# Hand-overs at the stage borders of an eight-stage fused kernel, and a new order of its last stage

## The chip, the cores and the metric

The kernel runs on one core of a Trainium2 chip. The metric is the device time of one execution in microseconds (us), as the median of several runs. The core has five engines that work beside each other, each through its own queue in order: TensorE (PE, matrix products into the accumulator memory PSUM), VectorE (DVE), ScalarE (ACT), GpSimd (POOL) and SyncE (SP, which here only issues DMAs).

## The reference

Input is x of 16 batches of 256 tokens with 128 features, in f32. Eight blocks follow each other, each with a norm before it, and a norm of its result that is added to x:

```python
x = x + _layernorm(_L0_attn_ref(_layernorm(x, axis=-1), ...), axis=-1)
x = x + _layernorm(_L0_ffn_ref(_layernorm(x, axis=-1), ...), axis=-1)
...
x = x + _layernorm(_L3_attn_ref(_layernorm(x, axis=-1), ...), axis=-1)
x = x + _layernorm(_L3_ffn_ref(_layernorm(x, axis=-1), ...), axis=-1)
```

L0 is one attention head and a gated MLP. L1's first half has four layers of local and linear attention with an FFN after each; its second half is a soft mixture of experts (2048 slots, softmax over slots and over tokens). L2 is causal attention and a GELU MLP. L3's first half is a selective scan, an MLP, grouped attention and a second MLP (root-mean-square norms ahead of each); its second half sends each batch's 64 best tokens per expert through 8 experts.

## The kernel before, in words

**Tiles.** The 4096 tokens lie as 8 groups (`NG`) of 512 tokens, two batches each; a group is a tile `x[g]` of 128 partitions x 4 x 128 f32, and x stays in SBUF from start to end. Work per group is written as a Python generator. A `yield` ends a turn of the generator; who runs next decides the order of the instructions in each engine's queue.

**Stages.** `program` calls seven stages, each in its own pools of SBUF and PSUM tiles: `stage_l0`; `stage_l1_attn` (L1's four layers, and in the last of them `fill`, which norms x for the next stage); `stage_soft_moe`; `stage_l2_attn`; `stage_trunk` (L2's MLP, the scan, L3's first MLP); `l3_gqa`; `stage_last` (L3's second MLP for each group, its closing norms, and the experts). A tile of a new pool can be used when the memory under it has been released by the stage before.

**Order.** Within `stage_l0`, the two attention stages, the trunk and the last stage the order is written by hand (`manual_schedule`): `Ctx.turns` (L373) runs items of (first turn, generator), one step of each per turn, in the order of the list. In the L1 stage and the soft mixture the program's own scheduler plans the queues from the traced order; there `Ctx.interleave` (L219) starts L1's 64 steps, a mix or an FFN of one group each, a step after the one before has had 4 (mix) or 2 (FFN) turns.

**Norms.** `Ctx.stats` (L247) takes mean and variance on DVE (bn_stats, bn_aggr, four of each per group) and 1/sqrt on POOL (L244, L245). `Ctx.normed` (L262) applies them with four DVE instructions. Two stages have a variant that applies them on ACT: POOL computes nb = -mean * rs (L577, L578; L1627, L1628), ACT computes x * rs + nb (L583, L1631).

**Stage borders.** In stage 0 every group ends with y (L719), its norm, the add to x, a second norm of x, z = normed x. L1 then begins: it fills its constant tiles on POOL (L746, L748), and the first mix norms z[0], transposes it and scales it (L776) to hT; products with hT follow. At the end of L1, `fill` stores x to DRAM and norms it on DVE into mxn. In the soft mixture the last pass `share` (L1145) collects two token blocks per group; then `end` divides by the sums (L1166, L1168), norms on DVE (mdisp) and adds the stored x back (L1170); it runs inside `share`, so the next block comes after it. The L2 attention starts with a norm of x[0] while POOL fills the value tiles (L344 to L349).

**The last stage.** `last(g)` squares xm[g] on POOL (L1638), sums on DVE (L1641), takes rsqrt on POOL, multiplies (n), transposes, goes through fc (Relu L1656, Square L1657) and proj, adds, norms twice, transposes and multiplies with the gate, and writes the probabilities. `selection(q)` finds the best tokens for four batches (two groups); `pair_of(q, pair)` gathers their tokens ("xin"), runs two experts and adds the results up ("sum"). The turns at which each starts stand in one list:

```python
    items = []
    for q in range(4):
        items += [(25 + 8 * q + 2 * pair, pair_of(q, pair)) for pair in range(4)]
    items = items[::-1] + [((19, 25, 33, 42)[q], selection(q)) for q in range(4)]
    items += [((0, 1, 3, 5, 7, 9, 19, 21)[g], last(g)) for g in range(NG)]
```

Of the kernel before, what the change touches and what calls it, by code (L numbers as in the profile page):

```python
# [21 lines left out]
F32 = mybir.dt.float32  # L22
I32 = mybir.dt.int32
BF16 = mybir.dt.bfloat16
AF = mybir.ActivationFunctionType
# [160 lines left out]
def idle(n):  # L186

    for _ in range(n):
        yield
# [10 lines left out]
class Ctx:  # L200
# [61 lines left out]
    def normed(self, out, src, mv, rs):  # L262
        for k in range(NT):
            self.nc.vector.tensor_scalar(
                out[:, k, :], src[:, k, :], mv[:, k, 0:1], rs[:, k : k + 1], ALU.subtract, ALU.mult
            )

# [275 lines left out]

def stage_l0(k, x, w, wv, wi, z):

# [10 lines left out]
    def constants():  # L556
# [12 lines left out]
        for name in f:  # L569
            v.tensor_scalar(f[name], wi[name], float(np.float32(1.0 / 127.0)), None, ALU.mult)  # L570
            yield

    def stats(src):

        mv, rs = k.stats(src)
        nb = k.t([P, NT], "ln_nb", 6)
        gp.tensor_scalar(nb, mv[:, :, 0], -1.0, None, ALU.mult)  # L577
        gp.tensor_tensor(nb, nb, rs, ALU.mult)  # L578
        return nb, rs

    def normed(out, src, nb, rs):
        for t in range(NT):
            nc.scalar.activation(  # L583
                out[:, t, :], src[:, t, :], AF.Identity, bias=nb[:, t : t + 1], scale=rs[:, t : t + 1]
            )

# [60 lines left out]

    def group(g):
        nb, rs = stats(x[g])
        yield from idle(2)  # L650
        xn = k.t([P, NT, D], "xn", 2)
        normed(xn, x[g], nb, rs)
        yield
# [36 lines left out]
        yield  # L690
        nb, rs = stats(x[g])
        yield from idle(2)
        xn = k.t([P, NT, D], "xf", 2)
        normed(xn, x[g], nb, rs)
        yield
# [21 lines left out]
        ps = k.tokens_ps(h, down)  # L717
        y = k.t([P, NT, D], "y", 3)
        nc.scalar.copy(y, ps)  # L719
        yield  # L720
        mv, rs = k.stats(y)
        yield from idle(2)
        k.normed(y, y, mv, rs)
        gp.tensor_tensor(x[g], x[g], y, ALU.add)
        yield
        nb, rs = stats(x[g])
        yield from idle(2)
        normed(z[g], x[g], nb, rs)
        yield

    with k.tc.manual_schedule():
        k.turns([(0, group(0)), (0, constants())] + [(4 * g, group(g)) for g in range(1, NG)])


def stage_l1_attn(k, x, ws, rows, z, then):

# [8 lines left out]
    for a in k.l1_val + k.l1_lin:  # L745
        nc.gpsimd.memset(a, 1.0)  # L746
    for a in k.l1_max + k.l1_ctx:
# [16 lines left out]
    for i in range(4):  # L764
        steps += [l1_mix(k, z[g], ws[i], rows[f"bo{i}"], NG * i + g) for g in range(NG)]
        steps += [ffn(i, g) for g in range(NG)]
        leads += [4] * NG + [2] * NG
    k.interleave(steps, 5, leads, -1)

# [26 lines left out]

def l1_mix(k, z, w, bo, n):

# [5 lines left out]
    tiles = lambda b: [slice((2 * b + t) * P, (2 * b + t + 1) * P) for t in range(2)]  # L804
    hT = yield from l1_norm_T(k, z, w["ln1_g"], w["ln1_b"])
    nc.gpsimd.tensor_tensor(z, z, bc(bo, 1, NT), ALU.add)
# [145 lines left out]
def soft_inputs(k, x, pool):  # L952

    xs = k.dram.tile([P, NG, NT, D], F32, tag="xs", name="xs")
    xn = [pool.tile([P, NT, D], F32, tag=f"mxn{g}", name=f"mxn{g}") for g in range(NG)]

    def fill(g):
        k.nc.sync.dma_start(out=xs[:, g], in_=x[g])
        yield from k.norm_to(xn[g], x[g])

    return xs, xn, fill


def stage_soft_moe(k, x, w, wdram, bdram, xn, xs):
# [157 lines left out]
    def share(n):  # L1122
# [3 lines left out]
        for b in range(NB):  # L1126
# [15 lines left out]
            for t in range(2):  # L1142
# [3 lines left out]
                else:  # L1146
                    v.tensor_copy(x[g][:, at, :], ps[:, t, 0:D])
            nc.scalar.copy(got[:, :, b], ps[:, :, D])  # L1148
            yield
            if n == blocks - 1 and b % 2:  # L1150
                yield from end(b // 2, f, got)
        if n == 0:
# [5 lines left out]
    def end(g, f, got):  # L1158

        back = k.t([P, NT, D], "slT", 3)  # L1160
        nc.sync.dma_start(out=back, in_=xs[:, g])
        bs = slice(2 * g, 2 * g + 2)
        r = k.t([P, 2, 2], "mend", 2)
        v.tensor_tensor(r, sums[:, :, bs], f[:, :, bs], ALU.mult)
        v.tensor_tensor(r, r, got[:, :, bs], ALU.add)
        v.reciprocal(r, r)  # L1166
        xg = x[g].rearrange("p (b t) d -> p b t d", b=2)
        v.tensor_tensor(xg, xg, bc(r.rearrange("p t b -> p b t"), 3, D), ALU.mult)  # L1168
        n = yield from k.norm(x[g], "mdisp", 3)
        nc.gpsimd.tensor_tensor(x[g], back, n, ALU.add)  # L1170

    for n in range(-2, blocks):
        parts = [
            share(n) if n >= 0 else None,
            logits(n + 2) if n + 2 < blocks else None,
            slots(n + 1) if 0 <= n + 1 < blocks else None,
        ]
        parts = [p for p in parts if p]
        while parts:
            parts = [p for p in parts if next(p, k) is not k]  # L1180


def stage_l2_attn(k, x, w, beside):
# [3 lines left out]
    def head(g, got):  # L1187
        yield
        xn = yield from k.norm(x[g], "xn", 1, 2)
        yield  # L1190
        ps = k.transposed_ps(xn)
# [325 lines left out]
def l3_gqa(k, xa, w, gain, first):  # L1517
# [31 lines left out]
    def tail(g, yT):  # L1549
# [5 lines left out]
        nc.gpsimd.tensor_tensor(xa[g], xa[g], y, ALU.add)  # L1555
        yield

    k.attention_stage(head, 26, 1, tail)
# [54 lines left out]
def stage_last(k, x, xm, w, xn, probs, out):  # L1613
# [9 lines left out]

    def normed(out, src, mv, rs):

        nb = k.t([P, NT], "ln_nb", 3)
        nc.gpsimd.tensor_scalar(nb, mv[:, :, 0], -1.0, None, ALU.mult)  # L1627
        nc.gpsimd.tensor_tensor(nb, nb, rs, ALU.mult)  # L1628
        yield from idle(2)
        for t in range(NT):  # L1630
            nc.scalar.activation(  # L1631
                out[:, t, :], src[:, t, :], AF.Identity, bias=nb[:, t : t + 1], scale=rs[:, t : t + 1]
            )

    def last(g):
        xg = xm[g]
        sq = k.t([P, NT, D], "rms_sq", 2)
        nc.gpsimd.tensor_tensor(sq, xg, xg, ALU.mult)  # L1638
        yield
        ss = k.t([P, NT], "rms_ss", 3)  # L1640
        v.tensor_reduce(ss, sq, AX.X, ALU.add)  # L1641
        rs = k.t([P, NT], "rms_rs", 3)
        k.rsqrt(rs, ss, 1.0 / D, RMS_EPS)
        yield from idle(2)
        n = k.t([P, NT, D], "n", 2)
# [19 lines left out]
        mv, rs = k.stats(y)  # L1665
        yield from idle(2)
        k.normed(y, y, mv, rs)
        nc.gpsimd.tensor_tensor(x[g], x[g], y, ALU.add)
        yield
        mv, rs = k.stats(x[g])  # L1670
        yield from normed(xn[g], x[g], mv, rs)
        yield
# [143 lines left out]
    for q in range(4):  # L1816
        items += [(25 + 8 * q + 2 * pair, pair_of(q, pair)) for pair in range(4)]
    items = items[::-1] + [((19, 25, 33, 42)[q], selection(q)) for q in range(4)]
    items += [((0, 1, 3, 5, 7, 9, 19, 21)[g], last(g)) for g in range(NG)]
    with k.tc.manual_schedule():  # L1820
# [4 lines left out]
def program(ctx: ExitStack, tc: tile.TileContext, xin, dram, at, out):  # L1825
# [45 lines left out]
    k.mhalf = base.tile([P, P], F32, tag="mhalf", name="mhalf")  # L1871
    nc.gpsimd.memset(k.mhalf, -0.5)
    rows1 = load_rows(base, "l1rows")

# [15 lines left out]
    z = [pz.tile([P, NT, D], F32, tag=f"z{g}", name=f"z{g}") for g in range(NG)]  # L1890
    stage("l0", "left", stage_l0, l0, l0v, l0f, z, banks=ONE_RING)
    closed("w0")
# [3 lines left out]
    xs, xn, fill = soft_inputs(k, x, psoft)  # L1896
    stage("l1a", "left", stage_l1_attn, l1, rows1, z, fill, banks=RING_BANKS)
    closed("z")
# [55 lines left out]
```

## Time and profile before

| what | us |
|---|---|
| median of three runs (2999.87 to 3004.17) | 2999.88 |
| the profiled execution | 3001.28 |
| its span | 2999.60 |
| PE busy in the span | 2756.1 (92%) |
| DVE, ACT, POOL busy | 1950.2, 1661.9, 1017.0 |

The stages by their first product on PE, in us of the span: L1 at 190, the soft mixture at 968, the L2 attention at 1564, the trunk at about 1881, the grouped attention at about 2380, the last stage at 2695; PE ends at 2988.

How to read the profile: the page lists busy time per engine and, in 40 slices of 75 us, busy tenths and the granted clock of PE (9 is full or nearly). A row of the timeline has start, length, engine, line, operation, output<-inputs and shapes; "[idle before <-releaser]" says how long the engine had stood and what let it go on. The chain of waits is followed back from the last instruction: each row is start, length, and what the end of the kernel waited for there. The helpers L317 (products) and L306 (transposes) stand for most PE rows; the tile's name says which product it is.

### The profile page before, as it was taken

How to read it: one execution, taken by the hardware profiler on the slowest of the kernel's cores; microseconds unless marked ns; L12 is line 12 of the kernel's file. 1: busy time of each engine (PE TensorE's matmuls, PEld its weight loads, DVE VectorE, ACT ScalarE, POOL GpSimd, SP SyncE). 2: the span in 40 equal slices, each digit the busy share in tenths (PEclk: the TensorE clock that was granted, in tenths of full speed). 3: DMA queues.
4: the chain of work that ended last, by engine and by line, in shares of the span. 5: the costliest groups of instructions: out<-in, count | busy, mean ns of one | idle time of the engine just before them, and what ended most of it. 6: DMA issues, size and time to landing. Idle time of an engine off the chain costs nothing.

```text
span 2999.6 us, 59389 instructions
## 1 busy us (share of the span) xinstructions
PE 2756.1 (92%) x23674; PEld 1881.2 (63%) x23674; DVE 1950.2 (65%) x5342; ACT 1661.9 (55%) x3488; POOL 1017.0 (34%) x1368
## 2 busy tenths in 40 slices
PE   8979999999997799999959998799999699978998
PEld 4547776777666588888843443466666344436897
DVE  5767466564667889999867775566674587735441
ACT  6745556455563667776725665344444277756543
POOL 3453333333335200000044555322231466644332
PEclk9989999999998899999979999899999799988999
DMA  4000000000001000000020000000000000010000
GB/s 115 12 1 2 1 2 2 1 2 1 2 2 37 1 12 12 8 9 9 9 73 1 1 1 1 1 1 1 1 1 1 2 1 1 1 42 16 2 15 15
DMA packets 29149, 31.29 MB, mean 10 GB/s; under 512 B 7292, under 2 KB 20156, under 8 KB 28732
## 3 DMA queue, kind: packets, MB, share of 16 engines
q1 hardware_dynamic: 28872, 27.49, 3.1%
q8 instruction: 187, 3.06, 0.4%
q14 instruction: 90, 0.74, 0.1%
HBM read 23.29 MB, written 4.19 MB: 9 GB/s over the span
## 4 chain that ended last, share of the span: by engine, by line
PE 51%; ACT 7%; DVE 6%; POOL 2%; issue 2%; DMA 0%; POOLq 0%; SPq 0%; ACTq 0%; DVEq 0%
PE ps_s L317 32%; PE ps_o L317 7%; PE ps_mm L317 6%; ACT at_e L472 1%; PE ps_s L306 1%; ACT lg L1129 1%; PE ps_xin L317 1%; ACT meT L1136 1%; PE ps_sum L317 1%; ACT mdisp L1036 1%; ACT lg L1009 1%; PE ps_s L506 1%; PE ps_t L1134 1%; DVE at_nm L440 1%; POOL ln_rs L245 1%
## 5 line engine op out<-in xcount | busy, mean ns | idle before, releaser
L244 POOL TENSOR_SCALAR ln_rs<-ln_mv 128x4 f32<-128x4 f32 x192 | 41.2, 215 | 879.6 <-DVE ln_mv L257 855.1
L440 DVE TENSOR_REDUCE at_nm<-ps_s 128x2 f32<-128x512 f32 (+1 forms) x384 | 238.1, 682 | 123.0 <-PE ps_s L317 123.0
L472 ACT ACTIVATE at_e<-ps_s 128x512 f32<-128x512 f32 x384 | 198.2, 603 | 93.3 <-PE ps_s L317 91.1
L1391 DVE TENSOR_TENSOR scan<-ps_s,lm 128x384 f32<-128x384 f32 x256 | 124.7, 549 | 143.1 <-PE ps_s L317 142.9
L478 POOL TENSOR_SCALAR_AFFINE_SELECT at_e<-at_e 128x1024 f32<-128x1024 f32 (+1 forms) x96 | 135.4, 1411 | 215.0 <-ACT at_e L472 214.7
L245 POOL TENSOR_TENSOR ln_rs<-ln_rs,mhalf 128x4 f32<-128x4 f32 x192 | 196.4, 1023 | 15.7
L854 DVE TENSOR_REDUCE l_max<-ps_s 128x3 f32<-128x384 f32 x256 | 124.1, 548 | 64.0 <-PE ps_s L317 64.0
L317 PE MATMUL ps_o<-my,meT 128*128 128x129 f32 x1024 | 145.6, 290 | 18.3 <-ACT mgot L1148 15.3
L317 PEld LDWEIGHTS ps_s<-l_w,mlp_h 128*128 128x128 f32 x1280 | 149.4, 192 | 18.8 <-issue 15.1
L317 PE MATMUL ps_s<-l1f_phi,mxT 128*128 128x256 f32 x512 | 141.5, 399 | 16.9 <-DVE mpart L1010 16.8
L317 PEld LDWEIGHTS ps_o<-my,meT 128*128 128x128 f32 x1024 | 128.8, 196 | 37.0 <-ACT mgot L1148 21.8
L317 PE MATMUL ps_s<-km,qT 32*128 32x512 f32 x768 | 140.0, 663 | 12.0 <-POOL km L364 10.5
L317 PE MATMUL ps_s<-l_w,mlp_h 128*128 128x128 f32 x1280 | 150.2, 275 | 0.3
L317 PE MATMUL ps_s<-qm,kT 32*128 32x512 f32 x768 | 144.2, 656 | 5.2 <-DVE at_nm L440 5.0
L904 POOL TENSOR_SCALAR_AFFINE_SELECT e<-e 128x512 f32<-128x512 f32 x128 | 78.8, 637 | 178.3 <-ACT e L901 178.3
L317 PE MATMUL ps_o<-at_e,at_vm 128*32 128x128 f32 (+1 forms) x2048 | 122.6, 336 | 15.3 <-ACT at_oT L502 15.3
L317 PE MATMUL ps_mm<-mdisp,mxn 128*128 128x128 f32 x1024 | 125.2, 278 | 5.0 <-DVE mdisp L1048 4.9
L901 ACT ACTIVATE e<-ps_s 128x384 f32<-128x384 f32 x256 | 105.5, 510 | 39.7 <-PE ps_s L317 39.6
L317 PEld LDWEIGHTS ps_mm<-mdisp,mxn 128*128 128x128 f32 x1024 | 121.6, 194 | 7.9 <-DVE mdisp L1048 6.6
L1368 ACT COPY BT<-ps_s 128x512 f32<-128x512 f32 x64 | 37.5, 586 | 154.6 <-PE ps_s L317 154.6
L317 PE MATMUL ps_s<-xT,l_w 128*128 128x512 f32 x256 | 119.3, 596 | 2.7 <-ACT mlp_h L789 2.7
L317 PEld LDWEIGHTS <-b_ident 128*128 128x128 bf16 x656 | 51.5, 98 | 110.0 <-issue 100.2
(427 smaller groups left out, 7083.9 us busy)
## 6 DMA issues: line engine op xcount, KB each, us to landing
mw<-in_l1fw SPq DMA_DIRECT2D x16, 256.0 KB, 2.7
moe_w<-in_moe SPq DMA_DIRECT2D x16, 256.0 KB, 5.3
l_w<-in_l SPq DMA_DIRECT2D x10, 256.0 KB, 3.4
x<-in_x SPq DMA_DIRECT2D x8, 256.0 KB, 4.6
xs<-x SPq DMA_DIRECT2D x8, 256.0 KB, 2.0
slT<-xs SPq DMA_DIRECT2D x8, 256.0 KB, 2.7
out<-x SPq DMA_DIRECT2D x8, 256.0 KB, 2.3
l1f_phi<-in_l1f SPq DMA_DIRECT2D x1, 1024.0 KB, 4.9
```

What stands on the lines that cost most here:

```text
L244: g.tensor_scalar(out, in_, scale, eps, ALU.mult, ALU.add)
L245: g.tensor_tensor(out, out, self.mhalf[:, :n], ALU.pow)
L306: self.nc.tensor.transpose(out[:n, k * P : (k + 1) * P], src[:, k, cols], self.c["ident"])
L317: self.nc.tensor.matmul(out, lhsT=lhsT, rhs=rhs, start=start, stop=stop, skip_group_check=True)
L440: v_.tensor_reduce(nm[:, t, r, vs], s, AX.X, ALU.max, negate=True)
L472: nc.scalar.activation(e[:, r], s, AF.Exp)
L478: nc.gpsimd.affine_select(at, at, [[0, 4], [0, n], [1, P]], ALU.is_ge, 0.0, base=0, channel_multiplier=-1)
L854: v.tensor_reduce(mx[:, b, :, h, 16], s, AX.X, ALU.max, negate=True)
L901: nc.scalar.activation(e[:, h].rearrange("p j n -> p (j n)"), s[:, : 3 * P], AF.Exp)
L904: nc.gpsimd.affine_select(e[:, :, j, :], e[:, :, j, :], [[0, 4], [1, P]], ALU.is_ge, 0.0, base=0, channel_multiplier=-1)
L1368: nc.scalar.copy(s, ps)
L1391: v.tensor_tensor(m, s[:, : SEQ + P], lm[:, SCAN_HEADS[4 * (t // 2) + 2 * i + hh], :], ALU.mult)
```

## The change

Three borders and the last stage are edited. The ACT form of the norm becomes a method of `Ctx`.

```diff
+    def stats_nb(self, src, kept=None):
+        mv, rs = self.stats(src)
+        g = self.nc.gpsimd
+        nb, to = kept or (self.t([P, NT], "ln_nb", 6), rs)
+        g.tensor_scalar(nb, mv[:, :, 0], -1.0, None, ALU.mult)
+        g.tensor_tensor(nb, nb, rs, ALU.mult)
+        if kept:
+            g.tensor_copy(to, rs)
+        return nb, to
+
+    def normed_act(self, out, src, nb, rs):
+        for t in range(NT):
+            self.nc.scalar.activation(
+                out[:, t, :], src[:, t, :], AF.Identity, bias=nb[:, t : t + 1], scale=rs[:, t : t + 1]
+            )
```

Stage 0 to L1: the last group stops at y, which is kept in a tile of its own; the rest of its stage 0 runs beside the first mix of L1. Group 0 also does its first L1 norm and transposes in stage 0. The fills of two kinds of constant tiles, three tiles of each, move from POOL to DVE.

```diff
-        y = k.t([P, NT, D], "y", 3)
+        y = y7 if g == NG - 1 else k.t([P, NT, D], "y", 3)
         nc.scalar.copy(y, ps)
         yield
+        if g == NG - 1:
+            return
...
+        if g == 0:
+            nb, rs = k.stats_nb(z[g])
+            yield from idle(2)
+            xn = k.t([P, NT, D], "xf", 2)
+            k.normed_act(xn, z[g], nb, rs)
+            yield
+            ps = k.transposed_ps(xn)
+            nc.scalar.activation(xT0, ps, AF.Identity, bias=l1["ln1_b"], scale=l1["ln1_g"])
+            yield
...
+def rest_of_l0(k, x, z, y):
+    yield from k.residual(x, y)
+    yield
+    nb, rs = k.stats_nb(x)
+    yield
+    k.normed_act(z, x, nb, rs)
...
     for a in k.l1_val + k.l1_lin:
-        nc.gpsimd.memset(a, 1.0)
+        nc.vector.memset(a, 1.0)
...
+    def beside(a, b):
+        for _ in a:
+            next(b, k)
+            yield
+
+    steps[0] = beside(steps[0], rest_of_l0(k, x[NG - 1], z[NG - 1], y7))
...
-    hT = yield from l1_norm_T(k, z, w["ln1_g"], w["ln1_b"])
+    if hT is None:
+        hT = yield from l1_norm_T(k, z, w["ln1_g"], w["ln1_b"])
```

L1 to the soft mixture: `fill` norms on ACT.

```diff
-        yield from k.norm_to(xn[g], x[g])
+        nb, rs = k.stats_nb(x[g])
+        yield
+        k.normed_act(xn[g], x[g], nb, rs)
```

The soft mixture to L2: `end` becomes a part of its own beside `share`; the division goes into the norm's factor; group 0's next statistics are taken here and kept, and L2 applies them on ACT.

```diff
-            yield
             if n == blocks - 1 and b % 2:
-                yield from end(b // 2, f, got)
+                parts.append(end(b // 2, f, got))
+            yield
...
-        v.reciprocal(r, r)
-        xg = x[g].rearrange("p (b t) d -> p b t d", b=2)
-        v.tensor_tensor(xg, xg, bc(r.rearrange("p t b -> p b t"), 3, D), ALU.mult)
-        n = yield from k.norm(x[g], "mdisp", 3)
-        nc.gpsimd.tensor_tensor(x[g], back, n, ALU.add)
+        rt = k.t([P, NT], "mendt", 3)
+        v.reciprocal(rt.rearrange("p (b t) -> p t b", b=2), r)
...
+        gp.tensor_tensor(rs, mv[:, :, 1], rt, ALU.mult)
+        gp.tensor_tensor(rs, rs, rt, ALU.mult)
+        k.rsqrt(rs, rs, 1.0, LN_EPS)
+        gp.tensor_tensor(rs, rs, rt, ALU.mult)
+        yield
+        n = k.t([P, NT, D], "mdisp", 3)
+        k.normed(n, x[g], mv, rs)
+        gp.tensor_tensor(x[g], back, n, ALU.add)
+        yield
+        if g == 0:
+            k.stats_nb(x[g], k.kept)
...
-        xn = yield from k.norm(x[g], "xn", 1, 2)
-        yield
+        if g == 0:
+            xn = k.t([P, NT, D], "xn", 1)
+            k.normed_act(xn, x[g], *k.kept)
+            yield from idle(3)
+        else:
+            xn = yield from k.norm(x[g], "xn", 1, 2)
+            yield
```

Grouped attention to the last stage: group 0's squares, their sums and the rsqrt are done at the end of that group's attention.

```diff
+        if g == 0:
+            ss = k.t([P, NT], "last_ss", 1)
+            sq = k.t([P, D], "last_sq", 1)
+            for t in range(NT):
+                nc.scalar.activation(sq, xa[g][:, t, :], AF.Square, accum_out=ss[:, t : t + 1])
+            yield
+            k.rsqrt(k.kept[0], ss, 1.0 / D, RMS_EPS)
```

The last stage: `last(0)` starts at the product with the kept factor; three pauses of two turns become one turn (after the rsqrt of the squares, after both statistics); and the list of turns is

```diff
-        items += [(25 + 8 * q + 2 * pair, pair_of(q, pair)) for pair in range(4)]
-    items = items[::-1] + [((19, 25, 33, 42)[q], selection(q)) for q in range(4)]
-    items += [((0, 1, 3, 5, 7, 9, 19, 21)[g], last(g)) for g in range(NG)]
+        items += [(23 + 8 * q + 2 * pair, pair_of(q, pair)) for pair in range(4)]
+    items = items[::-1] + [((16, 21, 30, 38)[q], selection(q)) for q in range(4)]
+    items += [((0, 0, 2, 3, 5, 7, 9, 11)[g], last(g)) for g in range(NG)]
```

## The prediction, made before the change had run

> **What bounds the kernel now.** I read the page's slices first, then the busy time in stretches of 5 us around each low slice, then the chain and the timeline inside those stretches. The page's rows for TensorE and its granted clock:
>
> ```profile
> PE   8979999999997799999959998799999699978998
> PEclk9989999999998899999979999899999799988999
> ```
>
> One digit is 75 us. PE is full nearly everywhere; what is lost lies in a few slices, and in the same slices the clock falls. So the time is PE's work plus the holes at the stage borders, and only holes can be won. Slice 3 (first border), by 5 us, is
>
> ```profile
> 175.00:180.00 5.00, 0.00 (x0) 0.00 (x0) 2.26 (x12) 0.48 (x2) 2.35 (x4) 0.72 0.01 2
> 185.00:190.00 5.00, 0.00 (x0) 0.00 (x0) 2.83 (x21) 0.00 (x0) 4.70 (x14) 0.50 0.00 0
> 195.00:200.00 5.00, 5.00 (x31) 3.17 (x29) 4.91 (x37) 2.10 (x3) 4.50 (x7) 0.74 0.00 0
> ```
>
> After the length of the stretch the columns are PE, its weight loads, DVE, ACT, POOL, the clock, and the DMA. PE stands from 172.6 (last matmul of stage 0) to 190.2 and then works at half clock until about 198. The timeline says why: group 7's chain of norm, add, norm lasts until 183.1; all tiles of the next stage start only then; five us of POOL fills precede the first rsqrt.
>
> The second border, 951 to 968, in the timeline:
>
> ```profile
> 954.87 1.26 POOL L284 TENSOR_TENSOR x<-x,ln_y 128x512 f32<-128x512 f32 x1
> 954.93 2.04 DVE L264 TENSOR_SCALAR mxn<-x,ln_mv,ln_rs 128x128 f32<-128x128 f32 x4 [0.26 <-POOL ln_rs L245]
> 966.08 1.11 DVE L264 TENSOR_SCALAR mxn<-x,ln_mv,ln_rs 128x128 f32<-128x128 f32 x4 [1.42 <-POOL ln_rs L245]
> ```
>
> PE ended its last FFN at 951.1, yet DVE adds that group's result only at 956.9: DVE is two groups late, and each group's mxn occupies it 2.04 us beside POOL's add (1.11 alone). The third border, in the chain:
>
> ```profile
> 1528.65 0.26 DVE x L1145
> ...
> 1529.23 1.24 DVE x L1168
> ...
> 1530.73 0.78 DVE ln_st L255 x4
> ...
> 1532.16 1.03 POOL ln_rs L245
> 1533.25 0.22 issue
> 1533.47 0.85 DVE mdisp L264 x3
> ...
> 1557.27 1.26 POOL x L1170
> ...
> 1562.53 0.99 POOL ln_rs L245
> ```
>
> The middle rows are one group's end. It repeats every 5.75 us (the rsqrt starts at 1526.41, 1532.16, 1537.90, 1543.65), all in series with the next blocks. The last two: the barrier at 1558.5 and the next stage's first norm, whose rsqrt stands behind POOL's fills. In the last stage PE has two holes: 2687.3 to 2695.0, where group 0's square, sum, rsqrt and product follow each other, and
>
> ```profile
> 2760.00:2765.00 5.00, 3.50 (x12) 2.52 (x12) 4.76 (x24) 1.89 (x6) 3.21 (x6) 0.50 0.01 2
> 2765.00:2770.00 5.00, 0.12 (x1) 0.13 (x1) 4.73 (x16) 0.70 (x2) 3.79 (x7) 0.50 0.00 0
> 2770.00:2775.00 5.00, 4.68 (x21) 3.92 (x21) 3.15 (x12) 2.61 (x9) 1.20 (x2) 0.50 0.00 0
> ```
>
> where groups 0 to 5 are through their MLPs and the experts wait for the first selection.
>
> **First border.** Group 7's chain goes beside the first mix; group 0's L1 norm and transposes go into stage 0. PE's first L1 matmul then needs only hT and PSUM, which the copy of y frees at 173.2. SBUF tiles open with the last of group 6, ACT's z at 175.5 instead of 183.1. PE could so start 19 us earlier (192.3 to 173.3). DVE is next: from 175.5 it has six fills (no DVE row; POOL's six take 3 x 0.57 + 3 x 0.31 = 2.6; ends 1.3 and 5; I take 2.6, the same elements), casts 0.6, group 7's two statistics and one norm (1.23 + 1.11 + 1.23 = 3.6), step 0's q 1.15, maxima 3.9 and the rest 2.1, step 1's norm 2.3 and q 1.15: 17.4, to 192.9. Before, step 1's q ended at 209.85, so 16.9; for waits in between I take 16.5 (ends 10 and 21). The fills, moved ahead of everything on DVE's queue, delay the maxima (PE waits for their banks); that is in the sum. With one turn less in step 0, step 1 starts one turn later against it; cover is the 3 us that PE needs for its projections.
> A rule to weigh: "TensorE: Matmul & The Clock Gate" in the Trainium skill (section "What's actually happening") holds that an idle window of about 3.4 us halves the clock and about 3.4 us of work restores it. By that this border's slow restart would cost 1.7 us; by the rows 190 to 200 it costs 3.87 x 0.5 + 5 x 0.26 = 3.2. I use the row; it is inside the 19.
>
> **Second border.** Eight mxn norms go from DVE to ACT: 8 x 2.04 us off DVE, 8 x 1.65 onto ACT (row L583, four in 1.65), and two POOL instructions more (0.23 + 0.20, 0.55 with the gap). After PE's end: add 0.7, statistics 1.2, POOL 1.25, norm 1.1, POOL add 1.26, statistics 1.2, POOL 1.25 + 0.55, ACT 1.65 = 10.2, to 961.3 against 967.2. Group 6's pieces lie between on DVE, so 5.0 (ends -1 and 6). "ScalarE: Activation LUTs" ("Rules for kernel authors") speaks against this: additions and multiplications belong on VectorE, and an ACTIVATE costs about 0.3 us plus 0.83 ns an element, an estimate of 1.6 for four. It is right about the instruction (1.65 against 1.11), and by it alone the border grows by 0.54 + 0.55 = 1.1 us. But the row shows DVE late by 5 us and ACT at 24 of 75 us there, so I follow the row. ACT's Gelu behind it waits up to 1.65 us once per group; in that slice ACT is idle two thirds.
>
> **Third border.** An end loses L1168 (1.24), and its POOL wait (1.44 with its issue) gets the next block's DVE work as cover: DVE's own work is 4 x 0.33 + 3 x 0.16 + 1.2 + 1.1 = 4.1; POOL 3.2 (three products more, 0.6); PE 3.4. I take 4.5 per group, since DVE and POOL block each other now and then (a 128x4 product took 1.12 beside POOL's add). The last rsqrt follows 7 x (5.75 - 4.5) = 8.8 us sooner; last chain about equal. So 9 (ends 3 and 11). SP's loads of xs go with the end into a later turn; behind them on SP wait only weights of later stages and two masks, 2 us to land, so nothing. Then head 0: statistics 1.2, rsqrt 1.0 behind fills, norm 1.3 go; ACT's norm takes 0.5 to the first transpose. POOL's fills (5.8) still end 5.8 after the barrier, and km needs POOL: scores 7.75 after it instead of 12.45: 4.7, of which 4.5. Together 13.5.
>
> **Last border and stage.** Four squares on ACT (no such row; nearest L583, 1.65; between 0 and 1.7) and a rsqrt move into the attention stage, where ACT is busy 55 of 75 us. The chain of POOL, DVE, POOL before the first product goes: 4.8 us sooner on PE. The MLPs: two more groups run in front at the front's rate, 60 us for six heads and three tails of some 51 us of PE work; by that, eight heads and five tails (70 us) take 80 from 2690.2, to 2770. Then the hole stays: the last group's remaining chain (copy 0.6, add 0.7, norm 3.6, add 1.3, norm 4.7, transposes and gate 2.3) is 13.2 us, and this gate stands ahead of the experts' first gather in PE's order, so that starts about 2784.5. After the first gather (2783.6 before) PE ran 203.9 us to 2987.5; 13.6 of that were groups 6 and 7 (one fc, two proj at 3.4, two tails at 1.7) and 1 a selection, so 189.3; the experts' start has no filler now, 4. End 2977.8: 9.7 sooner, I take 8 (ends 2 and 20), as ACT (three copies 1.8, Relu and Square 4 x 1.23, norm 1.65, p 0.4: 8.8 us a group) is as full as PE. The pauses cut from two turns to one cost nothing while a turn of the front lasts 4.4 us (proj starts at 2712.6, 2721.5, 2730.3, two turns apart); without that cover each group would wait 1.25 us for its rsqrt.
>
> **Added in the stages.** Group 0's early norm in stage 0: DVE 1.2, ACT 2.4, POOL 1.7, PE 0.6; covered by 22 of 75 us idle on DVE and 17 on ACT. With the squares 1.5 (ends 0 and 4; a gain is excluded, it is added work).
>
> **Sum.** 16.5 + 5 + 13.5 + 8 - 1.5 = 41.5. The profiled execution took 3001.28 (span 2999.60 and 1.68 around it), 1.4 above the median 2999.88; 3001.3 - 41.5 = 2959.8, on the median's scale 2958.
>
> **Rivals.** (1) As summed: 2958, own range 2947 to 2968, chance 0.60. (2) The hole before the experts closes, because sixteen turns at 5 us leave the selection finished and the first hot rows waiting: the last stage is worth 19, 2947; for it: selection needs two groups only; against: PE's order puts gate 7 first. 0.17. (3) DVE becomes the bound at the borders: fills and late norms push step 0's maxima, the ends run at 5 us: 9 + 3 + 6 + 3 - 1.5 = 19.5, 2980. For it: DVE is at 4.9 of 5 in 195 to 200. 0.16. (4) The release at a border still falls on the same last instruction, so nothing moves: 2998; against: group 7's chain leaves stage 0. 0.03. (5) Slower: L1's order is planned by the program, not written, and a changed start can spread through its 64 steps of (951 - 190)/64 = 11.9 us. A microsecond more per step gives 64 - 41.5 = 22 more, 3022; it turns slower from 0.75 a step. Against: only step 0 differs, and DVE has 47 of 75. 0.04.
>
> **Numbers.** Faster by over 0.2% (about what a measurement here can tell from no change): cases 1 to 3 and a shade, 0.93; within 0.03; slower 0.04. The range 2942 to 2976 leaves out the lower part of (2), half of (3), and (4) and (5): about 0.2.
>
> **What would show it.** PE's gap after stage 0 under 3 us, clock at 1.00 throughout, step 1's q near 193. The second barrier 10 us after PE's last FFN (16 before). Ends 4.5 us apart, no product of 128x512 in them. PE's first transposes of the last stage 1 us after the add; then still a hole near its turn 20. I am wrong if the stretches of L1's inside grow, or if the hole before the experts is gone.

## The result, and the profile after

The changed kernel takes 2980.07 us (median of 4 runs, 2973.4 to 2986.4) where the kernel before took 3000.74 on the same chip (2999.9 to 3004.2): a ratio of 0.9929, 95% interval 0.9905 to 0.9952. It is faster, by 21 us and not by the 41.5 of the forecast. Two later measurements of the same kernel on other chips gave 0.9941 (0.9926 to 0.9956) and 0.9963 (0.9951 to 0.9975), 19 and 11 us. The profiled execution took 2986.44 us (span 2984.7), the slowest of its four, 14.8 below the profiled 3001.28 of before; below, the place of a gain or a loss is read from traces, and its worth is held against the medians of several runs.

The page's rows for TensorE and its granted clock, after:

```profile
PE   8989999999998799999969998799999699989898
PEclk9989999999999799999978999899999799999899
```

The low slices are where they were, only less low: slice 3 (first border) has 8 instead of 7, slice 21 (third border) 6 instead of 5. The three stretches of the first border, in the columns used for before:

```profile
175.00:180.00 5.00, 4.46 (x33) 2.92 (x32) 3.36 (x15) 2.47 (x6) 2.22 (x6) 1.00 0.01 3
185.00:190.00 5.00, 4.06 (x26) 2.54 (x25) 4.94 (x25) 2.02 (x5) 2.40 (x6) 0.50 0.00 0
195.00:200.00 5.00, 5.00 (x13) 2.67 (x11) 3.28 (x15) 2.71 (x6) 3.69 (x5) 0.59 0.00 0
```

TensorE no longer stands: it is busy 4.46 of 5 where it had 0. But DVE is full (4.94 of 5), and the clock is at half from 182 to 199, where 1.00 was expected (a value between 0.50 and 1.00 is a mean over a change: by stretches of 1 us the clock is 1.00 up to 182, then 0.50 up to 199). Step 1's q was forecast to end at 192.9; it ends at 202.4. First TensorE's product that q is made of, then DVE's rows of step 1's norm, of a later step's norm and of q, and last the q of before:

```profile
198.65 2.12 PE L336 MATMUL ps_s<-l_tok,xT 128*128 128x256 f32 x8
```

```profile
190.46 1.29 DVE L264 TENSOR_SCALAR xn<-z,ln_mv,ln_rs 128x128 f32<-128x128 f32 x4 [0.26 <-POOL ln_rs L245]
...
198.39 1.76 DVE L264 TENSOR_SCALAR xn<-z,ln_mv,ln_rs 128x128 f32<-128x128 f32 x4 [1.72 <-POOL ln_rs L245]
...
202.09 0.27 DVE L867 TENSOR_TENSOR q<-ps_s,qm 128x128 f32<-128x128 f32 x1
```

```profile
209.56 0.29 DVE L832 TENSOR_TENSOR q<-ps_s,qm 128x128 f32<-128x128 f32 x1
```

The second border, last rows of POOL's, ACT's and DVE's timelines:

```profile
948.62 1.27 POOL L303 TENSOR_TENSOR x<-x,ln_y 128x512 f32<-128x512 f32 x1
...
954.85 1.81 POOL L1027 MEMSET mdisp<- 128x2048 f32 x1
```

```profile
952.98 1.65 ACT L283 ACTIVATE mxn<-x,ln_nb,ln_rs 128x128 f32<-128x128 f32 x4 [2.62 <-POOL ln_nb L275]
```

```profile
954.85 1.88 DVE L237 COPY mxT<-ps_t 128x512 f32<-128x512 f32 x1
```

TensorE's last FFN ended at 943.5, the barrier falls with ACT's last mxn at 954.6: 11 us instead of 16. Then DVE's first copy and POOL's fill start at the same instant, and the copy takes 1.88 us (the other three take 0.68 to 0.69).

The third border, in the chain of waits, with one whole end between two rsqrt and then the barrier:

```profile
1536.32 1.02 POOL ln_rs L245
...
1537.43 0.20 POOL ln_rs L1217
1537.63 0.03 issue
1537.66 1.11 DVE mdisp L264 x4
1538.77 0.52 DVE x L1182 x2
1539.29 0.84 DVE mend L1203
...
1541.41 0.21 POOL ln_rs L1214
...
1542.25 1.02 POOL ln_rs L245
...
1550.43 1.27 POOL x L1221
1551.71 0.03 issue
1551.73 0.50 ACT xn L283
```

The product of 128x512 is gone, and still the ends are 5.95 us apart (the rsqrt at 1524.41, 1530.37, 1536.32, 1542.25); before, 5.75. The norm follows the rsqrt chain at once, so DVE waits for POOL in every end. DVE's timeline shows all that it has to do between an end's statistics and its norm, two products, and then the wait (1.12 us in the ends of before):

```profile
1535.04 0.36 DVE L1212 BATCH_NORM_AGGREGATE ln_mv<-ln_st 128x2 f32<-128x6 f32 x4
1535.32 0.57 DVE L1182 SCALAR_TENSOR_TENSOR x<-x,mfade,ps_o 128x128 f32<-128x128 f32 x2
1537.66 1.11 DVE L264 TENSOR_SCALAR mdisp<-x,ln_mv,ln_rs 128x128 f32<-128x128 f32 x4 [1.77 <-POOL ln_rs L1217]
```

What the border did bring is the last row of the chain: ACT starts the next stage's first norm straight after the barrier.

At the start of the last stage TensorE's first transposes wait 2.74 us instead of 7.67 (before, then after):

```profile
2694.98 1.09 PE L306 MATMUL ps_s<-const_ident,n 128*128 128x128 f32 x4 [7.67 <-POOL rms_rs L244]
```

```profile
2684.25 1.12 PE L325 MATMUL ps_s<-const_ident,n 128*128 128x128 f32 x4 [2.74 <-DVE n L1705]
```

The hole before the experts is still there, as forecast:

```profile
2760.00:2765.00 5.00, 3.19 (x29) 2.96 (x27) 4.76 (x22) 1.53 (x4) 1.73 (x2) 1.00 0.00 0
2765.00:2770.00 5.00, 1.89 (x11) 1.74 (x11) 4.76 (x25) 2.05 (x6) 2.76 (x6) 0.59 0.00 0
2770.00:2775.00 5.00, 3.32 (x15) 2.74 (x15) 4.79 (x21) 1.87 (x6) 2.80 (x5) 0.50 0.00 2
```

And there is a hole that before did not have, in the grouped attention (ACT's timeline):

```profile
2473.91 2.05 ACT L491 ACTIVATE at_e<-ps_s 128x512 f32<-128x512 f32 x4
2478.40 0.31 ACT L1622 ACTIVATE last_sq<-xm 128x128 f32<-128x128 f32 x1 [2.44 <-POOL xm L1615]
...
2480.12 1.28 ACT L1556 ACT_TABLE_LOAD   x1
2481.41 0.31 ACT L1556 ACTIVATE ss<-ss 128x128 f32<-128x128 f32 x1
2481.74 1.28 ACT L491 ACT_TABLE_LOAD   x1
2483.03 2.06 ACT L491 ACTIVATE at_e<-ps_s 128x512 f32<-128x512 f32 x4
```

The first square waits 2.44 us for POOL's addition; behind it in ACT's queue stand two table loads and the exponentials that TensorE needs. The kernel before has the two loads as well, but there the same two at_e rows start 6.45 us apart; here 9.12:

```profile
2482.67 2.05 ACT L472 ACTIVATE at_e<-ps_s 128x512 f32<-128x512 f32 x4
...
2489.12 2.06 ACT L472 ACTIVATE at_e<-ps_s 128x512 f32<-128x512 f32 x4
```

TensorE has 2.95 and 2.32 of 4 us busy there (2478 to 2486), and its clock falls to half (0.58 in the second of the two stretches).

How the traces are compared below: of an instruction that both kernels have, its time in the profiled execution of before less its time in the other is its *advance*. A border is worth the advance behind it less the advance ahead of it (for the first border: from stage 0's last silu to the second mix). That is needed because executions differ: at 53 us, ahead of every change, the advance lies between -0.1 and 4.2 us already. The traces show where that comes from. The clock's record holds only 1.00 and 0.50, in all twenty traces, and inside the kernel each stretch at half lasts 3.4 us or a whole multiple of it; so one of them costs 1.7 us where TensorE is the bound. In before and in the five traces with an advance under 0.5 the record of full clock begins at 26.0 to 27.0 us, in the fourteen others at 13.6 to 15.7 (the same four products, wkT by wqT at 15.1 us, take 2.07 us in before and 1.13 in after), and the six of these with only 2.5 to 2.9 fall to half once more, for 3.4 us at 21.

### The profile page after: what moved, and what is told of

It is laid out like the page before. It is cut to its first block, busy times and chain, and to the rows that moved or that the text cites. A ratio compares the mean times of both kernels' runs of the same rounds, so it can differ in the third digit from the quotient of the medians.

```text
span 2984.7 us, 59424 instructions
## 1 busy us (share of the span) xinstructions
PE 2762.0 (93%) x23673; PEld 1885.7 (63%) x23674; DVE 1937.7 (65%) x5299; ACT 1673.2 (56%) x3532; POOL 1023.6 (34%) x1406
## 4 chain that ended last, share of the span: by engine, by line
PE 75%; ACT 11%; DVE 8%; POOL 3%; issue 3%; DMA 0%; POOLq 0%; SPq 0%; ACTq 0%; DVEq 0%
PE ps_s L336 52%; PE ps_o L336 8%; PE ps_mm L336 6%; PE ps_s L325 2%; ACT at_e L491 1%; POOL ln_rs L245 1%; ACT lg L1166 1%; PE ps_xin L336 1%; ACT meT L1173 1%; PE ps_sum L336 1%; DVE ln_st L255 1%; ACT mdisp L1073 1%; ACT lg L1046 1%; PE ps_t L1171 1%; PE ps_s L973 1%
## 5 line engine op out<-in xcount | busy, mean ns | idle before, releaser
L336 PE MATMUL ps_o<-my,meT 128*128 128x129 f32 x1024 | 147.1, 291 | 21.2 <-ACT mgot L1185 17.1
L336 PEld LDWEIGHTS ps_s<-l_w,mlp_h 128*128 128x128 f32 x1280 | 149.4, 192 | 18.8 <-issue 15.1
```

The lines of the kernel that those rows point to most:

```text
L336: self.nc.tensor.matmul(out, lhsT=lhsT, rhs=rhs, start=start, stop=stop, skip_group_check=True)
```

## The experiments

**The four parts, each alone on the kernel before.** All four ran on one chip (before: 2997.23 us, median of 64 runs). The edit is the part's own hunks of the diff.

First border alone.

> The kernel before with the first border of the change alone (group 7's chain beside step 0, group 0's hT made in stage 0, fills on DVE). Theory T, from the trace after (the terms of the sum are mis-sized, each by itself): 8.5 us faster than before, since step 0 has one turn less, step 1 starts a turn later against it, and 6 us of the 14.5 that step 0 wins are lost by step 1. Rival R (each part alone is worth what was predicted, and the parts take it from one another): 16.5 us faster.

Measured: 2991.6 us, ratio 0.9981 (0.9974 to 0.9988), 5.6 us faster: below T's 8.5 and a third of R's 16.5. In its trace the border is worth 7.2 (advance 1.13 at stage 0's last silu, 8.33 from the second mix on); ahead of it stage 0 loses 1.7 where group 0's early norm runs (advance 2.87 at 92 us, 1.13 at 130): TensorE waits 2.64 us there, 1.30 in before, for exponentials that now stand behind the early norm's copy in ACT's queue. All sixteen traces with this part lose 1.7 or 3.4 us there (the five with 3.4 have the clock at half for 3.4 us from 117), the three of parts without it 0.0; and 7.2 - 1.7 = 5.5 is near the 5.6 of the medians.

Second border alone.

> The kernel before with the second border alone (mxn normalised by ACT). T: the barrier comes 4 to 5 us earlier, but the first copies of mxT on DVE then lie beside POOL's fill of 1.8 us, so 1.5 to 2 us faster in all. R: 5 us faster.

Measured: 2992.81 us, 0.9986 (0.9979 to 0.9992), 4.4 us faster; advance 2.65 in L1, 6.96 in the soft mixture, so 4.3. R's 5 nearly holds, not T's 2: the slow copy beside POOL's fill is there too, but costs little behind the barrier.

Third border alone.

> The kernel before with the third border alone (ends of the soft mixture a turn later and without the product of 128x512; group 0's norm from kept statistics). T: the ends stay at 5.8 to 6.0 us per group, since DVE waits for a POOL chain of five small instructions; only the first head is won, 4.8 us, of which some goes again: 2 to 4 us faster. R: ends at 4.5 us per group, 13.5 us faster.

Measured: 2993.37 us, 0.9988 (0.9980 to 0.9996), 3.9 us faster; advance -0.5 in the soft mixture, 1.8 in L2's attention, 2.3. T: the ends are 5.95 us apart here as well.

Last border and stage alone.

> The kernel before with the last border and the last stage alone (squares in the attention stage, MLPs in front, experts from turn 23). T: 9 us faster, the hole before the experts stays. R: the squares cost the attention stage 3 us (its end was 3 us less ahead than its beginning in the trace after), so 6 us faster, and the attention stage of this run is 3 us longer than before's.

Measured: 2998.74 us, 1.0004 (0.9997 to 1.0010): no gain. Neither number came out; of R it holds that the squares cost the attention stage something, 5.1 for its 3. The trace splits it: advance -1.57 before group 0's squares in the grouped attention and -6.70 behind them, 5.1 lost in one place; then -9.2 at the stage's end, +0.48 in the experts, 9.7 for the last border and stage. Of these 9.7 some 3 belong to before's execution: the three other parts, which change nothing there, win 2.7 to 3.4 over the same stretch. That leaves 6.3 to 7. The rest went at the ends of the two attention stages (2.6 us each), where the clock fell in this execution. The edit does not reach the first of them, and at the second the changed kernel itself won 1.5 us in one execution and lost 2.6 in another. Whether other executions of this part lose there too, one trace cannot show.

So the four add up to 12.4 us by the medians, and nothing in them says that the parts take their gain from one another: the whole gave 11 to 21.

**The changed kernel again, and three repairs.** On a second chip (before: 3002.28).

> The changed kernel once more, unaltered, for a time on the same chip as the other runs and a second trace. The holes in its first trace at 115 to 140 us of stage 0 should be gone if they belonged to that execution; the hole at 2478 to 2490 in the grouped attention, where TensorE's clock fell to 0.57, should be there again if the four squares make it. Faster than before by 18 to 21 us.

Measured: 2983.53 us, 0.9941, 18.8 faster. The hole at the squares is there again (advance 13.77, then 8.63). Of those in stage 0 the one by 115 is there again too: it is group 0's early norm. So is the loss of 1.7 us at 137 to 141, one stretch at half clock; the third border alone, which has no early norm, shows one at 135 to 138, so it is not that norm's work.

Lead of the first step, the turns that L1's loop waits before it starts the next one:

```
         leads += [4] * NG + [2] * NG
+    leads[0] = 3
```

> The changed kernel with the first lead of L1's order at 3 turns instead of 4, so that step 1 starts as many turns after step 0's work as before the change. Theory T (the turn that step 0 lost delays step 1, and this alone makes the first border worth 8.5 instead of 14.5 us): 5 to 6 us faster than the changed kernel, step 1's catT 13 us or more earlier than in the kernel before. Rival (DVE is the bound there: fills, maxima, group 7's norm): under 1.5 us faster.

Measured: 2980.58 us, 3 faster than the changed kernel and inside the spread. The second mix has an advance of 7.62 (7.59 without the edit), while the *first* mix fell from 13.56 to 7.62. My theory of the late turn is wrong: the first mix had been ahead for nothing. Step 1's q ends at 201.1 here, 1.4 us earlier, and the border is worth the same 8.6; so q alone does not set it.

The squares four turns later, in the grouped attention's tail:

```
         if g == 0:
+            yield from idle(4)
             ss = k.t([P, NT], "last_ss", 1)
```

> The changed kernel with the four squares of the grouped attention four turns later, when POOL's add is long done. T (ACT stood 2.4 us behind the squares' wait for POOL's add, and its two table loads, Sqrt and Exp came late by that and the 1.7 us of squares, so TensorE stood and lost its clock: 4.7 us in all): 3 to 5 us faster than the changed kernel, no hole at 2480. Rival (the squares' own work on a full ACT is the price): 0 to 1 us faster, the hole only moves.

Measured: 2978.61 us, 4.9 faster than the changed kernel. The advance across the place is 13.62, then 13.63, and 13.24 behind the squares' new place: 0.4 is lost instead of 5.1. The same four squares run, so what cost nearly 5 us was the wait and what stood behind it, not their work.

The ends a turn longer, newest first:

```
-                parts.append(end(b // 2, f, got))
+                parts.insert(1, end(b // 2, f, got))
...
         gp.tensor_tensor(rs, rs, rt, ALU.mult)
-        yield
+        yield from idle(2)
         n = k.t([P, NT, D], "mdisp", 3)
```

> The changed kernel with the ends of the soft mixture one turn longer and the newest end first, so that between a group's statistics and its norm DVE has two products of the shares and the next group's statistics. T (an end is 5.95 us because DVE waits 1.8 us for POOL's five instructions): ends 4.3 to 4.8 us apart, 8 to 12 us faster than the changed kernel. Rival (DVE and POOL block one another in any order, or TensorE and ACT set the pace of the shares): ends over 5.5 us apart, under 3 us faster.

Measured: 2968.34 us, 15 faster than the changed kernel (more than the 8 to 12 expected), 0.9891 (0.9875 to 0.9907) of before. One end in its chain of waits:

```profile
1521.42 1.00 DVE mdisp L264 x4
1522.42 1.04 DVE x L1182 x4
1523.46 0.02 issue
1523.48 0.17 ACT mgot L1185
1523.66 1.26 DVE mend L1204
1524.92 0.20 DVE ln_st L1210
...
1525.57 0.28 DVE ln_mv L1212 x4
1525.85 1.00 DVE mdisp L264 x4
```

POOL has left the chain; an end lasts 4.43 us (the forecast had 4.5), though the product of 128x4 (mend, L1204) now takes 1.26 us beside POOL's addition, 0.14 alone. The border is worth 13.4 us (advance 9.8 to 23.15); the forecast had 13.5. In the four later traces with this edit it is worth 13.3 to 16.4. Which of the edit's two halves does it, the longer turn or the order, was not tried apart.

**What holds the first border back.** On a third chip (before: 2997.06), with group 7's chain begun later:

```
-        for _ in a:
-            next(b, k)
+        for n, _ in enumerate(a):
+            if n > 3:
+                next(b, k)
             yield
```

> The changed kernel with group 7's chain beside step 0 begun four turns later, so that on DVE step 0's first maxima and step 1's statistics and norm stand ahead of it. After the miss with the lead the theory is now T2: what step 1 waits for is DVE's queue (group 7's norm ahead of the maxima lets TensorE stand 2.4 us at 181, its clock falls to 0.50 until about 198, and step 1's norm comes only at 190.5). T2: TensorE's clock stays above 0.9 or falls only briefly, step 1's q ends at 195 to 198 instead of 202.4, 4 to 6 us faster than the changed kernel. Rival R2 (the sum of DVE's work up to there is what counts, in any order, the statistics for steps 2 to 6 in it): under 1.5 us faster.

Measured: 2987.35 us, 0.9969 (0.9956 to 0.9981): no gain, rather 3 us lost against the run that follows. The border is worth 5.5. TensorE's wait of 2.4 us at 181 shrank to 0.59, and the clock fell to 0.50 all the same. Step 1's q ends at 198.3, but stage 0 had ended 3.2 us earlier in this execution. T2 falls.

The fills back on POOL (`nc.gpsimd.memset(a, 1.0)`):

> The changed kernel with the six fills of val and lin back on POOL, 2.4 us off the front of DVE's queue. R2 (DVE's sum is the bound): step 1's q about 2.4 us earlier and 2 us faster than the changed kernel. T2 (order): 0 to 1 us, and if POOL's fills push the rsqrt of group 7 and with it the maxima behind it on DVE, up to 3 us slower.

Measured: 2984.58 us, 0.9954 (0.9941 to 0.9967); the border is worth 8.6, as in the traces that leave this border as changed (7.2 to 9.4). It neither helps nor harms: what DVE saves it waits, since group 7's first rsqrt now stands behind the fills on POOL, and DVE waits 3.23 us for it instead of 0.68.

The ends and the squares together, and with the chain of group 7 later as well:

> The changed kernel with both repairs together, the ends a turn longer and newest first, and the squares four turns later. Theory: the two losses are independent, so 15 + 5 = 19 to 21 us faster than the changed kernel, about 2964. Rival (what one wins the other loses at a later border): under 17.

> The changed kernel with three repairs, the ends, the squares and group 7's chain four turns later. T2: 23 to 26 us faster than the changed kernel, 37 to 44 faster than before, near the 2958 that was predicted for the change. R2: as without the third repair, 19 to 21 us faster than the changed kernel.

Measured: 2966.05 us (0.9892, 0.9879 to 0.9905) and 2971.69 us (0.9907, 0.9892 to 0.9921). The first is 18.5 us below the run with the fills on POOL, the nearest to the changed kernel on that chip: just under the 19 to 21. In its trace both gains are there (16.3 at the third border, 0.3 lost at the squares instead of 5). The medians do not show that they add: as a ratio the ends alone already had 0.9891. The third repair takes 5.6 us away again (5.9 for the first border instead of 9.4).

On a fourth chip (before: 2998.36) the clock was to be held up by matmuls without use, and DVE's work was cut:

```
-        for _ in a:
+        o = k.ps("o")
+        for n, _ in enumerate(a):
             next(b, k)
+            for _ in range({2: 2, 4: 3}.get(n, 0)):
+                k.mm(o, ws[0]["wq"], xT0)
             yield
```

> The changed kernel with five matmuls of 128x512 without use on TensorE in step 0 of L1, two between the first and the second half of the scores, three behind the linear part, where it stood 2.4 and 2.8 us. C (the clock is the cause): the clock stays at 1.00 through 180 to 200, the loss by slow clock between 168 and 240 falls from 7 or 8 us to under 2, and the kernel is 3 to 7 us faster than the changed kernel. D (DVE's work is the cause): TensorE only waits longer elsewhere, within 1.5 us.

Measured: 2980.78 us, against 2987.8 for the changed kernel on that chip. The stretches of 4 us and, from DVE's timeline, step 1's norm and q:

```profile
182.00:186.00 4.00, 2.66 (x29) 1.89 (x30) 4.00 (x17) 2.08 (x9) 1.27 (x1) 1.00 0.00 2
186.00:190.00 4.00, 3.68 (x20) 1.58 (x20) 4.00 (x20) 1.90 (x5) 2.33 (x6) 1.00 0.00 0
```

```profile
190.52 1.29 DVE L264 TENSOR_SCALAR xn<-z,ln_mv,ln_rs 128x128 f32<-128x128 f32 x4 [0.43 <-POOL ln_rs L245]
...
202.15 0.27 DVE L870 TENSOR_TENSOR q<-ps_s,qm 128x128 f32<-128x128 f32 x1
```

The clock stays at 1.00 until 192.6, but is at half again from there to 196.0 and from 202.8 to 209.6; the loss by slow clock falls to 4.7 us, not under 2. Even so q is a test of C, for only 3.4 us at half clock are left ahead of it instead of 17: step 1's q comes at 202.15, and in the second trace of the changed kernel, whose first fill on DVE starts at the same time (176.59 against 176.60), it comes at 202.15 too. The product that q is made of is done 2.0 us earlier than in the first trace (198.74 for 200.77), but q stands on DVE behind the later step's norm in both. In the trace the border is worth 7.5, no more than without. So the traces speak against C at this border. The 7 us between the two medians are C's 3 to 7 all the same, and above D's 1.5; the two ratios' intervals overlap (0.9930 to 0.9957 and 0.9951 to 0.9975), the traces do not show where the 7 us would come from, and the changed kernel had nearly this ratio (0.9941 for 0.9943) itself on another chip, so I leave them open.

Group 7's chain left out (z of group 7 is a copy):

> The changed kernel without group 7's chain beside step 0: its residual norm, its addition to x and the norm that makes z are left out (z of group 7 is a copy of y), 3.6 us of DVE and three rsqrt of POOL. D: step 1's q 3 to 4 us earlier and 3 to 4 us faster than the changed kernel. C: under 1.5 us, if the clock falls all the same.

> The changed kernel, unaltered, on this chip, as the reference for the other three: 15 to 21 us faster than before.

Measured: 2985.03 and 2987.8 us. Without the chain step 1's q is 2.5 us earlier, measured from the end of stage 0, and the border is worth 10.7 instead of 7.2 on this chip (8.5 in the second trace). That is somewhat less than D's 3 to 4 us, and so are the 2.8 us between the medians. The edit takes work off DVE and two rsqrt and an addition off POOL at once; with the fills on POOL, less work on DVE alone had brought nothing.

> The filled gaps together with the two repairs that helped (ends a turn longer and newest first, squares four turns later). C: 3 to 7 us faster than those two alone, which were 18.5 us faster than the changed kernel on one chip: 21 to 26 us. D: 17 to 20 us.

Measured: 2965.88 us, 0.9896 (0.9882 to 0.9909): 22 us below the changed kernel there, which is in C's range, but as a ratio no better than the two repairs alone (0.9892), and in its trace the first border is worth 7.2. I read that, and those 7 us, as spread; it is not shown.

Last, on a fifth chip (before: 2999.48), the order of L1's first twelve turns as written, by `held = self.tc.manual_schedule()` entered ahead of the loop in interleave and left at turn 12; the second run has the two repairs as well:

> The changed kernel with the order of L1's first twelve turns as written instead of as planned: on DVE step 1's q and first maxima stand ahead of the statistics of steps 2 to 5. D2 (those statistics, 7.7 us of DVE with their waits, held q back): step 1's q 5 to 7 us earlier than 202.4, 4 to 6 us faster than the changed kernel. L (what counts is when step 1's norm comes, 190.5, and the chain behind it through TensorE and ACT): q at most 2.5 us earlier, within 2.5 us; slower, if the later steps' norms now come late.

> The same on top of the two repairs that helped (ends, squares). D2: 4 to 6 us faster than those two alone, which were 0.9892 of before: about 0.9875. L: 0.988 to 0.990.

Measured: 2990.01 us (0.9957, 0.9944 to 0.9971) and 2972.25 (0.9908, 0.9895 to 0.9922); the border is worth 1.6 and 2.8. DVE's timeline:

```profile
191.28 1.29 DVE L270 TENSOR_SCALAR xn<-z,ln_mv,ln_rs 128x128 f32<-128x128 f32 x4
198.11 0.29 DVE L872 TENSOR_REDUCE qm<-ps_s 128x8 f32<-128x128 f32 x1 [5.53 <-PE ps_s L342]
...
199.29 0.29 DVE L873 TENSOR_TENSOR q<-ps_s,qm 128x128 f32<-128x128 f32 x1
202.07 1.95 DVE L895 TENSOR_REDUCE l_max<-ps_s 128x3 f32<-128x384 f32 x4 [2.48 <-PE ps_s L342]
```

With nothing between norm and q, DVE stands 5.53 us for step 1's transposes, copy and projections (with the clock at half up to 195.9). The q is 2.8 us earlier, a little more than L's 2.5 and far from D2's 5 to 7, but the later steps' norms come late, and the second run is just above L's 0.988 to 0.990. L holds in the main: what the planner puts in that gap fills a wait that is there anyway.

## Why the forecast was wrong, step by step

**What bounds the kernel** was right: the inside of L1 kept its advance within about 0.4 us over its 64 steps (rival 5 did not come), so the gain lies in the borders alone.

**First border: 16.5 forecast, 7.2 to 9.4 measured in the traces.** The failed step is "step 1's norm 2.3 and q 1.15: 17.4, to 192.9". Up to the norm the sum comes out, in part by luck: the terms up to there (16.25) from the forecast's 175.5 give 191.75, where the norm does end, but the fills start 1.0 us later than forecast, at 176.5, and the work takes 1.0 less. But q does not follow the norm: between them lie the transposes, their copy and three projections, 5.5 us of wait when DVE has nothing else (half clock for most of it), and in the planned order the norms of later steps as well. The q ended at 202.4. I compared a 209.85 that has this chain in it with a 192.9 that has not. The clock, expected at 1.00, fell to half: by TensorE's busy time in stretches of 4 us from 168 to 240, times what its clock lacks to 1, that took 6.9 to 9.1 us in the changed kernel's three traces, where the rows of before gave 3.2 for the restart and the estimate from the rule of "TensorE: Matmul & The Clock Gate" in the Trainium skill (section "What's actually happening") 1.7. But it was not what held q: with 3.4 us at half clock ahead of it instead of 17, q came at the same instant. The fills were sized right (2.4 for 2.6), and moving them back brought nothing. Clock, chain and DVE's queue cover one another here; only leaving out group 7's chain helped. Full clock and held order together were not tried, so what sets the rest of this border's worth stays open.

**Second border: 5.0 forecast, 4.4 and 4.3 measured.** The row of the trace was the right one to follow against the rule of "ScalarE: Activation LUTs" in the Trainium skill (section "Rules for kernel authors"): ACT's four norms take 1.65 us, near the 1.6 estimated from its figures, and the border still shrank from 16 us to 11.

**Third border: 13.5 forecast, about 2 measured** (from the middle of the soft mixture to L2's attention: 2.3 in the part alone, 1.9 to 2.4 in most traces with the changed kernel's ends, -0.3 in two, which lose some 1.5 inside the soft mixture ahead of the ends). Head 0 is as forecast: scores 7.6 us after the barrier (7.75 forecast). The failed step is "its POOL wait gets the next block's DVE work as cover": as the turns are written, two products of 0.57 us together are all that lies between an end's statistics and its norm, while POOL's chain grew from two instructions to five (2.1 us). That the mechanism itself was sized right, the run with the newest end first shows: 4.4 us per end, 13.4 for the border (13.3 to 16.4 in five traces).

**Last border and stage: 8 forecast, 9.6 to 9.8 measured against before's trace in all but one of the sixteen traces that have it, 6 to 7 against kernels without it.** TensorE waits 4.9 us less ahead of its first transposes, for the 4.8 forecast; the hole before the experts stayed, so rival 2 did not come.

**Added work: 1.5 forecast, 6.3 and more measured.** Group 0's early norm took 1.7 us in stage 0 (3.4 in the five traces with a stretch at half clock there), more than the whole of the forecast; the squares another 4.6 to 5.4, and 0.3 to 0.4 where they come later. The failed step is "four squares on ACT ... between 0 and 1.7". I costed the instructions and not their wait: one turn behind POOL's addition they reach ACT 2.44 us before it is done, and two table loads and the exponentials stand behind them.

The sum of the traces, 8.5 + 4.3 + 2 + 9.7 - 6.7 = 17.8, or 14.5 with 6.4 for the last stage, lies among the 11, 19 and 21 us that the whole kernel showed. The first time fell on rival 3's 2980, but that is luck, for rival 3 is only half true: DVE's queue holds q at the first border, with the chain close behind; in the ends DVE and POOL wait for each other; at the second border DVE is not the bound; and rival 3 knows nothing of the squares.

The change with the two repairs took 2966.05 us against 2997.06 of before on its chip, 0.9892 (0.9879 to 0.9905), 31 us less, with the third border at or above its forecast and the first still short. By its ratio the repair of the ends alone (0.9891) cannot be told from it.

## What to carry to other kernels

A wait is covered only by what stands between the two instructions in the engine's own order: write down that list for each hidden wait, before it is costed at nothing. An instruction moved to an engine with room is paid by the queue behind it, if its input comes late: ask when the input lands, not only how long the instruction lasts. And of a border's time, compare the same event with the same chain on both sides; the first mix came 14 us earlier here and the second only 8.

## What was not expected of the hardware

- Small products on DVE beside an addition of 128x512 on POOL: 128x4 took 0.93 to 1.27 us, 0.14 alone, and ended with the addition (1524.92 and 1524.89 in the run with the newest end first). A copy of 128x512 from PSUM on DVE took 1.88 us when it started together with POOL's fill of 128x2048, 0.68 when it started 0.17 us ahead of it; but a cast of 128x128 that had started 0.14 us ahead of that fill took 2.02 us, 0.23 in before. So the head start is not shown to be the cause.
- TensorE's clock went to half at 179.1 in the run with group 7's chain later, though no wait in the 8 us ahead of it was longer than 0.7 us (2.89 of 4 us busy from 174 to 178, 3.98 from 178 to 182). Once down, it stayed at half for 13.7 us there, and for 17.1 in the trace after, in which TensorE was busy 11.8 and 13.8 us.
- Single executions of one kernel differ by up to 4 us at a border, with the clock at half for longer in one than in the other: at the grouped attention's end (2650 to 2695) the same kernel had 1.5 us more and 2.6 less than before, with 10 and 20 us at half clock. The three parts of 4 to 6 us could be told from nothing with 13 to 21 runs.
